# A cross-attention block on one core: two heads' scores per ScalarE instruction, some maxima on VectorE alone, fewer folded sums, and another written-out order

## The chip, the cores and the metric

The kernel runs on 1 core of a Trainium2 chip. The metric is device time in microseconds (us), the median of several executions of the whole program.

## The reference

A transformer block with cross-attention on 8 batch rows of 256 tokens, 256 keys per row, width 512, 16 heads of 32, inner width 2048, all in fp32. The mask is all ones in the inputs, but is applied.

```python
x = layer_norm(hidden, ln1_w, ln1_b)
q, k, v = x @ q_w + q_b, enc @ k_w + k_b, enc @ v_w + v_b
scores = where(mask, einsum('bhqd,bhkd->bhqk', q, k) / sqrt(32), lowest)
out = einsum('bhqk,bhkd->bhqd', softmax(scores), v) @ cproj_w + cproj_b
hidden = out + hidden
y = layer_norm(hidden, ln2_w, ln2_b)
result = hidden + gelu(y @ fc_w + fc_b) @ proj_w + proj_b
```

## The kernel before, in words

**Stages.** The eight rows are two groups `g` of four rows (1024 tokens). Each group goes through: context and input turned to feature-major layout (`c`, `x`), the projections `k`, `v`, `q`, attention in 16 units, the output projection `o`, second layer norm `y`, the first MLP product `fc`, GELU, the second MLP product `pd`. Stages of the two groups overlap.

**Products.** Every large product is done by seven products of half-size blocks (a Strassen scheme, `quad`; in the MLP, one inside the other). The products go to PSUM banks named `X`, `Y`, `W` of the quad, and other engines add them up: `L601` and `L606` copy a bank out, `L625` adds a bank to an SBUF tile. The block sums that feed them (`c0t`, `fw0i`, `z1i` and so on) are also `L625` and `L623`, on VectorE (DVE) or GpSimd (POOL). All matrix products are issued at L634; transposes by TensorE (PE) at L722, the last four at L1322.

**Attention.** A unit is one row and four heads. `scores` (its name in the program is `s` and three digits: group, four heads, row) makes 8 small matmuls, 2 chunks of 128 keys by 4 heads; a head has 32 rows, so four of them share the PE array ("row" mode). Each head's result lies in a PSUM bank of its own, two chunks of 256 columns. ScalarE (ACT) then copies the 8 pieces of 256 columns to SBUF, each with the mask as bias (`ev`, L614), into two tiles `pr` of two heads. DVE takes the maximum over the keys with a reduction that transposes 32x32 blocks (`mx`, L1033, one for each `pr`); the rest of the maximum goes over three small ACT copies (`mc`, L1039), a DVE reduction (`fold`, L1040) and a DVE transpose (`mf`, L1042), then through DRAM and back, spread over all partitions (`md`, `mm`). `less` subtracts it (POOL at L1057 in two instructions, or DVE at L1053 in one), `exp` is ACT at L1060.

Softmax sums come from a matmul with `ones`. `attend` (`av` and the digits) does it and the product with `v` in one op of small matmuls ("col" mode, four heads share the array). A unit's kind decides how: kind `z` first adds the two chunks of keys (`ss`, L625, POOL or DVE, twice 128x512) and needs 4 `ones` matmuls, kind `p` skips `ss` and needs 8. With 8 matmuls for `v` that is 12 or 16. `KINDS` gives the kind of the 16 units of each group. `inverse` and `scale` (L1083, L1085, L1086, L625) end the unit.

**Order.** Nothing is scheduled by the compiler. `PROGRAM` is a list of some 3000 words, an op each, with a letter for the engine where there is a choice (V is DVE, A is ACT, G is POOL); each engine executes its ops in that order, and waits on semaphores for what others make. `PLACES` gives the slot of SBUF or PSUM of each buffer. All DMAs are issued by SyncE (SP) in one row, loads at L588 and stores at L594.

**Start and end.** Before the first data come in, 12 small matmuls of constants (`first`, L646) are run, and 4 more (`small`) between the first transposes and the first product. At the end, the last quad's fourth product (`pd_V`) is added to an output tile on DVE (`oz`), and SP stores it (`st01`). The other rows of the second group go out in tiles `tq` of 64 KB a store (`so1`), after DVE transposes (L1349) and an addition (`out1`, L625).

**Bias.** `xb` (L1428) adds the bias of the output projection to an input tile, one instruction of 1024 columns, on POOL or DVE.

Of the kernel before, what the change touches and what calls it, by code (L numbers as in the profile page):

```python
# [127 lines left out]
rows5 c0_30:A eps_x0_1 v0_0_P2 rows4 rows6 fw0_10_0 c0t4:V v0_1_t2:V v0_0_t3:A pow_x0_1 nb_x0_1 norm_x0_11:A mk kw11
rows8 v0_1_P2 fw0_00_1 v0_0_P3 kws3:V mk~1 fw0i4_3:G fw0_10_1 cols fw0_00_0 xt0_5 v0_1_P5 fw0i4_2:V xt0_6 fw0i4_4:V
kws1:V kws2:V cols~1 k0_0_t1:A k0_1_t1:V xt0_0 k0_1_P6 v0_0_c11 xt0_7 fw0_01_0 fw0s3:V v0_1_t3:A xt0_1 fw0s1:G  # L130
fw0i5_1:G v0_1_c11 stats_x0_31 k0_0_P7 stats_x0_21 k0_1_t2:A fw0i5_2:G kw01 xt0_4 fw0_01_1 fcd0_5_False fcd0_7_False
stats_x0_00 fw0i5_3:V fw0i1_1:V fcd0_4_True fw0i7_1:G fw0i1_3:V k0_0_P6 qw00 k0_0_t2:A aggr_x0_00 fw0i7_2:V fw0i7_4:V
# [1381 lines left out]
```

## Time and profile before

| what | value |
|---|---|
| median of 3 runs (lowest to highest) | 652.07 us (650.86 to 652.34) |
| the profiled execution | 651.16 us |
| its span, first to last instruction | 649.4 us |
| PE busy | 643.4 us |
| DVE busy | 577.5 us |
| ACT busy | 346.5 us |
| POOL busy | 392.8 us |
| granted TensorE clock, mean | 1.000 |
| data moved by DMA | 144.83 MB |

Busy is the time in which an engine executes something. A matmul's end is modelled: each fp32 matmul is two instructions in the profile, and while they follow each other without a gap their modelled times overlap, so the start of one to the start of the next is the time that it takes. An idle engine costs nothing unless the last instruction waits for it. "av<-ss,ones" is an instruction that writes av and reads ss and ones; `x16` after a row is the number of instructions in it.

### The profile page before, as it was taken

To read this page: it belongs to the slowest core of one execution; us is meant where nothing else is said; L and a number is where in the kernel's file an instruction comes from. 1 tells how busy PE (TensorE), PEld (TensorE's weight loads), DVE (VectorE), ACT (ScalarE), POOL (GpSimd) and SP (SyncE) were. 2 spreads that over 40 slices of the span, in tenths; PEclk is the share of its full clock that TensorE was granted. 3 is DMA by queue.
4 is the path that set the end of the run, shared out by engine and by line. 5 is a ranking of instruction groups with operands and counts; after the bars stand their busy time and mean duration, and the time that the engine had idled before them with its cause. 6 is when DMAs were issued, how large, how long until landed. Compare 5 with 4: busy or idle time off the path is not lost.

```text
span 649.4 us, 11225 instructions
## 1 busy us (share of the span) xinstructions
PE 643.4 (99%) x3793; PEld 486.6 (75%) x3793; DVE 577.5 (89%) x985; ACT 346.5 (53%) x709; POOL 392.8 (60%) x351
## 2 busy tenths in 40 slices
PE   9999999999999999999999999999999999999997
PEld 7755464477545776787788888888888888888886
DVE  4889998999899999999999999988878777999975
ACT  2244698999999989966864746120130222523000
POOL 2643676869987997698949746325823266321244
PEclk9999999999999999999999999999999999999999
DMA  8999998668764457777877887899988989577665
GB/s 271 300 353 301 249 250 297 227 204 151 217 224 142 140 199 232 261 255 247 254 222 225 248 255 257 276 328 159 165 213 193 234 184 217 143 194 225 174 139 97
DMA packets 206713, 144.83 MB, mean 223 GB/s; under 512 B 117136, under 2 KB 167104, under 8 KB 206656
## 3 DMA queue, kind: packets, MB, share of 16 engines
q1 hardware_dynamic: 206656, 144.11, 77.9%
q8 instruction: 30, 0.49, 0.3%
q14 instruction: 27, 0.22, 0.1%
HBM read 104.10 MB, written 39.98 MB: 222 GB/s over the span
## 4 chain that ended last, share of the span: by engine, by line
PE 93%; ACT 4%; POOL 1%; DMA 1%; issue 0%; DVE 0%; ACTq 0%
PE pd_X L634 15%; PE fc_X L634 15%; PE pd_W L634 7%; PE fc_W L634 7%; PE av L634 7%; PE s L634 5%; PE q_X L634 4%; PE o_X L634 4%; PE v_X L634 4%; PE k_X L634 4%; PE fc_Y L634 4%; PE pd_Y L634 4%; PE v_W L634 2%; PE k_W L634 2%; PE o_W L634 2%; ACT pr L614 2%
## 5 line engine op out<-in xcount | busy, mean ns | idle before, releaser
L614 ACT ACTIVATE pr<-s,cols 128x256 f32<-128x256 f32 x256 | 102.9, 485 | 10.4 <-PE s L634 7.8
L1057 POOL TENSOR_TENSOR pr<-pr,mm 128x512 f32<-128x512 f32 x70 | 90.5, 1327 | 5.8 <-DMA mm<-md 5.7
L1237 ACT ACTIVATE h<-h,cols 128x256 f32<-128x256 f32 x128 | 55.2, 499 | 61.1 <-DVE h L625 45.0
L1033 DVE TRANSPOSE_TENSOR_REDUCE mx<-pr 128x32 f32<-128x1024 f32 x64 | 77.1, 1219 | 1.9 <-ACT pr L614 1.7
L1060 ACT ACTIVATE pr<-pr 128x1024 f32<-128x1024 f32 x64 | 66.5, 1061 | 11.2 <-POOL pr L1057 8.1
L625 DVE TENSOR_TENSOR h<-fc_X,h 128x512 f32<-128x512 f32 x80 | 52.5, 675 | 6.2 <-PE fc_X L634 4.9
L625 POOL TENSOR_TENSOR ss<-pr 128x512 f32<-128x512 f32 x24 | 31.5, 1322 | 14.7 <-ACT pr L1060 11.9
L625 DVE TENSOR_TENSOR h<-fc_W,h 128x512 f32<-128x512 f32 x48 | 32.0, 677 | 4.8 <-PE fc_W L634 4.1
L1053 DVE TENSOR_TENSOR pr<-pr,mm 128x1024 f32<-128x1024 f32 x29 | 35.9, 1252 | 0.0
L1039 ACT COPY mx<-mx 32x64 f32<-32x64 f32 x96 | 23.8, 249 | 14.6 <-DVE mx L1033 13.3
L623 POOL TENSOR_TENSOR z1t<-h,z1t 128x512 f32<-128x512 f32 x6 | 8.0, 1359 | 26.1 <-DMA pl<-prd 12.3
L625 POOL TENSOR_TENSOR tq<-tq,rq 128x512 f32<-128x512 f32 x8 | 10.2, 1274 | 20.7 <-DMA rq<-hd 14.4
L634 PE MATMUL pd_X<-z0i,pl 128*128 128x256 f32 x96 | 22.5, 379 | 0.0
L634 PE MATMUL fc_W<-y1i,fl 128*128 128x256 f32 x84 | 20.7, 379 | 0.0
L634 PE MATMUL pd_W<-z1i,pl 128*128 128x256 f32 x88 | 20.6, 379 | 0.0
L625 DVE TENSOR_TENSOR h<-fc_Y,h 128x512 f32<-128x512 f32 x24 | 15.9, 673 | 5.3 <-PE fc_Y L634 5.3
L634 PEld LDWEIGHTS pd_X<-z0i,pl 128*128 128x128 f32 x96 | 18.2, 190 | 2.5
L601 ACT COPY h<-fc_X 128x512 f32<-128x512 f32 x16 | 9.0, 594 | 18.5 <-PE fc_X L634 15.6
L634 PE MATMUL pd_X<-h,pl 128*128 128x256 f32 x80 | 18.9, 379 | 0.0
L811 POOL TENSOR_TENSOR rs_y<-rs_y,neg_half 128x2 f32<-128x2 f32 x8 | 10.3, 1292 | 14.2 <-DMA pl<-prd 7.7
L634 PEld LDWEIGHTS pd_W<-z1i,pl 128*128 128x128 f32 x88 | 16.7, 190 | 2.3
L625 DVE TENSOR_TENSOR po<-pd_X,po 128x256 f32<-128x256 f32 x24 | 9.9, 414 | 9.6 <-PE pd_X L634 9.5
(574 smaller groups left out, 1847.0 us busy)
## 6 DMA issues: line engine op xcount, KB each, us to landing
pl<-prd SPq DMA_DIRECT2D x65, 256.0 KB, 3.6
mm<-md SPq DMA_DIRECT2D x32, 512.0 KB, 4.2
fl<-fcd SPq DMA_DIRECT2D x40, 256.0 KB, 4.2
fw<-in_L_xattn_fc_w_dram SPq DMA_DIRECT2D x16, 256.0 KB, 3.5
hid<-in_x_dram SPq DMA_DIRECT2D x8, 512.0 KB, 6.1
pw<-in_L_xattn_proj_w_dram SPq DMA_DIRECT2D x32, 128.0 KB, 3.7
hd<-hid SPq DMA_DIRECT2D x8, 512.0 KB, 4.9
fcd<-fw0i SPq DMA_DIRECT2D x7, 512.0 KB, 6.3
```

The source lines that it names most:

```text
L601: (nc.scalar.copy if e == "ACT" else nc.vector.tensor_copy)(to(), of_())
L614: lambda e: nc.scalar.activation(to(), of_(), AF.Identity, bias=bias(), scale=1.0))
L623: nc.gpsimd.tensor_tensor(to()[:, ts(k, 512)], in0()[:, ts(k, 512)], in1()[:, ts(k, 512)], op)
L625: E[e].tensor_tensor(to(), in0(), in1(), op)
L634: nc.tensor.matmul(o(), l(), r(), start=first, stop=True, skip_group_check=True)
L811: lambda e, rs=rs: nc.gpsimd.tensor_tensor(tile_of(rs)[:, 2:4], tile_of(rs)[:, 0:2], neg_half[:, 0:2], ALU.pow), lock=True)
L1033: T.op(f"mx{u}_{h}", [("DVE", 1.126)], [(pr[h], None)], [(mx, [h])], lambda e, h=h: nc.vector.tensor_reduce(tile_of(mx)[:, 0:256].rearrang ...
L1039: lambda e, a=a: nc.scalar.copy(*(tile_of(mx)[p : p + 32, 0:256].rearrange("p (c m) -> p c m", m=8)[:, :, m : m + 2] for p, m in ((0, 2 * ...
L1053: nc.vector.tensor_tensor(p_, p_, m_[:, None, :].to_broadcast([P, 2, 512]), ALU.subtract)
L1057: E[e].tensor_tensor(p_, p_, m_, ALU.subtract)
L1060: lambda e, h=h: nc.scalar.activation(tile_of(pr[h]), tile_of(pr[h]), AF.Exp), table="exp")
L1237: lambda e, f=f, b=b, c=c: nc.scalar.activation(at(h[f][b], c), at(h[f][b], c), AF.Gelu_apprx_tanh, bias=col(c_fcb + f * 4 + c), scale=1.0 ...
```

## The change

1. PSUM is taken as four pairs of banks. A unit's scores lie in two pairs (kind `D`), and one ACT instruction takes the same chunk of both heads of a pair, 512 columns in two banks: 4 instructions (`ew`) for each unit in place of 8 (`ev`). Buffers `X`, `Y`, `W` and the like use one half of a pair, so in the lists of the changed kernel their tile has the name of the first buffer that used the pair (`ps_c0_21` where an `av` or a `k` quad is meant). `by_bank` tells the framework which instructions meet in which bank, so that the two halves of a pair do not wait for each other.
2. `MAXIMA` names 16 of the 32 units (letter v) whose maximum is finished on DVE alone: a reduction 128x32, four transposes 32x32 and a reduction 32x32, in place of 3 ACT copies, a reduction and a transpose.
3. `KINDS`: 8 units are of kind `z` in place of 16.
4. `xb` on POOL is two instructions of 512 columns; `small` writes a PSUM buffer of its own.
5. `PROGRAM` and `PLACES` are new throughout.

```diff
-SLOTS = {"Q": (45, 1024), "P": (36, 512), "H": (14, 256), "sm": (10, 32), "mx": (3, 352)}
-BANKS = ("W", "C")
+SLOTS = {"Q": (45, 1024), "P": (36, 512), "H": (14, 256), "sm": (14, 32), "mx": (3, 352)}
+BANKS = ("W", "C", "D")
...
 PROGRAM = """
-cq0_00_0 turn_c0_10_0 turn_c0_00_0 vw00 c0_10_0:A c0_00_0:V small v0_0_P1a cq0_00_1 turn_c0_00_1 c0_00_1:A cq0_01_1
+cq0_00_0 small vw00 turn_c0_10_0 c0_10_0:V turn_c0_00_0 c0_00_0:A v0_0_P1a cq0_00_1 turn_c0_10_1 turn_c0_00_1 v0_0_P1b
...
-KINDS = ("zzzzzzzzzzpppppp", "ppppppppppzzzzzz")
+KINDS = ("zppzpppzpzpppppp", "pppppppppppzpzzz")
+MAXIMA = ("vaavavvavvvvavvv", "vavvaaaavvaaaaaa")
...
+            elif b.kind == "D":
+                b.t = banks.tile([P, 1024], F32, tag=f"D{b.slot // 2}", name=b.name)
+                pairs[b.slot // 2] = None
             else:
-                b.t = banks.tile([P, 512], F32, tag=f"B{b.slot}", name=b.name)
+                s, k = divmod(b.slot, 2)
+                if pairs.get(s) is None:
+                    pairs[s] = banks.tile([P, 1024], F32, tag=f"D{s}", name=b.name)
+                b.t = pairs[s][:, ts(k, 512)]
...
-        sb = [Buf(f"s{u}_{j}", "C", 2) for j in range(4)]
+        sb = [Buf(f"s{u}_{h}", "D", 2) for h in range(2)]
...
-            for j in range(4):
-                copy(f"ev{u}_{j}{kc}", (pr[j // 2], [2 * kc + j % 2]), (sb[j], [kc]), lambda j=j, kc=kc: at(pr[j // 2], 2 * kc + j % 2),
-                     lambda j=j, kc=kc: at(sb[j], kc), 256, lambda kc=kc: col(2 * (4 * g + b) + kc))
+            for h in range(2):
+                two = lambda t: t.rearrange("p (j n) -> p j n", j=2)
+                copy(f"ew{u}_{h}{kc}", (pr[h], [2 * kc, 2 * kc + 1]), (sb[h], [kc]), lambda h=h, kc=kc, two=two: two(at(pr[h], 2 * kc, 2)),
+                     lambda h=h, kc=kc: tile_of(sb[h]).rearrange("p (j k n) -> p j k n", j=2, k=2)[:, :, kc], 512,
+                     lambda kc=kc: col(2 * (4 * g + b) + kc))
...
+        def fold(e):
+            t = tile_of(mx)
+            nc.vector.tensor_reduce(t[:, 64:96], t[:, 0:64].rearrange("p (k c) -> p c k", k=2), axis=mybir.AxisListType.X, op=ALU.max)
+            for a in range(4):
+                nc.vector.transpose(t[0:32, 96 + 32 * a : 128 + 32 * a], t[32 * a : 32 * a + 32, 64:96])
+            nc.vector.tensor_reduce(t[0:32, 320:352], t[0:32, 96:224].rearrange("p (a r) -> p r a", a=4), axis=mybir.AxisListType.X, op=ALU.max)
...
-            T.op("small", [("PE", 0.1)], [], [], lambda e: small(WARM2))
+            ps = Buf("ps_small", "C")
+            T.op("small", [("PE", 0.1)], [], [(ps, None)], lambda e: small(WARM2, tile_of(ps)))
...
+    def biased(e, h):
+        if e == "DVE":
+            v = tile_of(h).rearrange("p (i n) -> p i n", i=2)
+            nc.vector.tensor_tensor(v, v, cb.t[:, None, :].to_broadcast([P, 2, D]), ALU.add)
+            return
+        for i in range(2):
+            nc.gpsimd.tensor_tensor(at(h, i, 1, 512), at(h, i, 1, 512), cb.t, ALU.add)
```

Three places of the new order that matter below, each engine's own list.

TensorE, the product of unit 020 with `v` (op `av020`), before; the names `k1_0_Y` and the like are PSUM banks of a key projection.

```order
L634 MATMUL k1_0_Y_1043<-c1_10_967,vws2_291 128x512 x2
L634 MATMUL k1_1_X_985<-c1t2_1049,vw11_255 128x512 x2
L634 MATMUL k1_0_X_956<-c1t2_1049,vw11_255 128x512 x2
L634 MATMUL av020_1079<-ss020_1066,ones_89 32x256 x4
L634 MATMUL av020_1079<-pr020_0_794,v0_0_21_333 32x256 x2
L634 MATMUL av020_1079<-pr020_1_788,v0_0_21_333 32x256 x2
L634 MATMUL av020_1079<-pr020_0_794,v0_0_21_333 32x256 x2
L634 MATMUL av020_1079<-pr020_1_788,v0_0_21_333 32x256 x2
```

TensorE, the same op in the changed kernel; the bank has the name `ps_c0_21` of the pair's first user.

```order
L621 MATMUL ps_c0_21_270<-c1_10_850,kw01_410 128x512 x2
L621 MATMUL ps_c0_10_0_213<-c1t2_935,v0_0_21_312 128x512 x4
L621 MATMUL ps_c0_21_270<-pr020_0_751,ones_89 32x256 x2
L621 MATMUL ps_c0_21_270<-pr020_1_767,ones_89 32x256 x2
L621 MATMUL ps_c0_21_270<-pr020_0_751,ones_89 32x256 x2
L621 MATMUL ps_c0_21_270<-pr020_1_767,ones_89 32x256 x2
L621 MATMUL ps_c0_21_270<-pr020_0_751,v0_0_21_312 32x256 x2
L621 MATMUL ps_c0_21_270<-pr020_1_767,v0_0_21_312 32x256 x2
L621 MATMUL ps_c0_21_270<-pr020_0_751,v0_0_21_312 32x256 x2
L621 MATMUL ps_c0_21_270<-pr020_1_767,v0_0_21_312 32x256 x2
```

The `ones` matmuls read the scores `pr` themselves and are 8 where they were 4, and no `ss` is awaited; the op follows the same quad as before.

ScalarE, the scores of unit 020 leaving PSUM, before, up to the three small copies for its maximum.

```order
L614 ACTIVATE pr020_1_788<-s020_2_769,cols_87 128x256 x2
L614 ACTIVATE pr020_0_794<-s020_0_765,cols_87 128x256
L614 ACTIVATE pr020_1_788<-s020_3_771,cols_87 128x256 x2
L614 ACTIVATE pr020_0_794<-s020_1_767,cols_87 128x256 x2
L614 ACTIVATE pr020_0_794<-s020_0_765,cols_87 128x256
L606 ACTIVATE q0_1_21_742<-q0_1_X_650,cols_87 128x512
L606 ACTIVATE xt0_5_395<-q0_0_X_627,cols_87 128x512
L1039 COPY mx020_807<-mx020_807 32x32x2 x3
```

ScalarE, the same in the changed kernel.

```order
L601 ACTIVATE pr020_0_751<-s020_0_727,cols_87 128x512 x2
L601 ACTIVATE pr020_1_767<-s020_1_730,cols_87 128x512 x2
L593 ACTIVATE q0_1_22_770<-ps_c0_10_0_213,cols_87 128x512
L593 ACTIVATE kw01_410<-ps_c0_21_270,cols_87 128x512
L1042 COPY mx020_754<-mx020_754 32x32x2 x3
```

Eight instructions of 256 columns became four of 512, and all of one pair of heads leave before the other pair.

SyncE, the end of its list before, 64 KB stores from `tq` tiles and then the three last ones.

```order
L594 DMA out_0_dram<-tq1_1_5735 32x16x32
L594 DMA out_0_dram<-tq1_0_5633 32x16x32 x3
L594 DMA out_0_dram<-tq1_1_5735 32x16x32 x3
L594 DMA out_0_dram<-tq1_0_5633 32x16x32 x2
L594 DMA out_0_dram<-tq1_1_5735 32x16x32 x3
L594 DMA out_0_dram<-pl12_3_5631 128x2x256
L594 DMA out_0_dram<-ot0_5819 128x2x128 x2
```

SyncE, the end of its list in the changed kernel. The fifth store of the first row is the first of the half tile that `out1_10` makes, an addition that was on DVE and is on POOL now.

```order
L581 DMA out_0_dram<-tq1_1_5365 32x16x32 x5
L581 DMA out_0_dram<-tq1_0_5309 32x16x32
L581 DMA out_0_dram<-tq1_2_5299 32x16x32
L581 DMA out_0_dram<-tq1_0_5309 32x16x32
L581 DMA out_0_dram<-tq1_1_5365 32x16x32
L581 DMA out_0_dram<-tq1_0_5309 32x16x32
L581 DMA out_0_dram<-tq1_1_5365 32x16x32
L581 DMA out_0_dram<-tq1_3_5305 32x16x32
L581 DMA out_0_dram<-tq1_1_5365 32x16x32
L581 DMA out_0_dram<-tq1_0_5309 32x16x32
L581 DMA out_0_dram<-ot0_5448 128x2x128
L581 DMA out_0_dram<-tq1_0_5309 32x16x32
```

Two more rows follow, the 256 KB store from `pl14_3` and the last 128 KB store from `ot0`. Between the wait for POOL and the last store stand 12 other stores.

More of the change, by code (lines that the diff above doesn't have):

```diff
@@ L128 @@
[L128 to L132, printed above, removed]
@@ L1035, in scores @@
+            T.op(f"mx{u}_{h}", [("DVE", 1.126)], [(pr[h], None)], [(mx, [h])], lambda e, h=h, put=put: nc.vector.tensor_reduce(
+                put(),
                 tile_of(pr[h]).rearrange("p (n r) -> p n r", r=32), axis=mybir.AxisListType.X,
                 op=ALU.max, apply_transpose=True))
[L1037 to L1039 removed]
@@ L1467, in tile_xattn_block, with place, meet, by_bank @@
     proj(1, h1)
+    def place(b):
+        return {("Q", b.slot // 2, h) for h in (0, 1)} if b.kind == "Q" else {("Q", b.slot // 2, b.slot % 2)} if b.kind == "P" else {(b.kind, b.slot)}
+    def meet(o, d):
+        if d in o.deps:
+            return True
+        return any(a is not b and place(a) & place(b) for a in o.bufs for b in d.bufs
+                   if a.kind in SLOTS and b.kind in SLOTS)
+    KNOWN = mybir.DependencyInfo(mybir.DependencyClass.Sync, mybir.DependencyReason.DATA)
+    past = {}
+    def by_bank(o, made):
+        for b in {b for b, _ in o.touched if b.kind in BANKS and b.kind != "D"}:
+            tile_of(b)
+            pair, k = pairs[b.slot // 2], b.slot % 2
+            name = pair.tensor.name
+            mine = [i for i in made if any(
+                getattr(x, "bass_ap", None) is not None and x.bass_ap.tensor.name == name and x.bass_ap.offset % 1024 // 512 == k
+                for x in list(i.ins) + list(i.outs))]
+            writes = (b, True) in o.touched
+            written, read = past.setdefault((name, k), ([], []))
+            others = [(d, j) for d, j in past.get((name, 1 - k, "all"), []) if d.eng != o.eng]
+            kept = [j for d, j in others if meet(o, d)]
+            for i in mine:
+                for d, j in written + read:
+                    if d.eng != o.eng:
+                        tc.add_manual_dep(i, j.name, KNOWN, reason="same bank")
+                for d, j in others:
+                    if d in o.deps:
+                        tc.add_manual_dep(i, j.name, KNOWN, reason="operands")
+                for e in ENGINES:
+                    if e != o.eng:
+                        tc.declare_no_dep(i, group=f"{name}_{1 - k}{e}", keep=kept, reason="the pair's other bank")
+            for i in mine:
+                tc.add_to_no_dep_group(f"{name}_{k}{o.eng}", i)
+                past.setdefault((name, k, "all"), []).append((o, i))
+            last = [(o, i) for i in mine[-(4 if o.mode in ("row", "col") else 1):]]
+            if writes:
+                past[name, k] = (last, [])
+            else:
+                read.extend((o, i) for i in mine)
     order = T.run()
@@ L1471, in tile_xattn_block @@
         for o in order:
+            n = len(nc.cur_bb.bb.instructions)
             o.fn(o.eng)
+            if any(b.kind in BANKS for b in o.bufs):
+                by_bank(o, list(nc.cur_bb.bb.instructions)[n:])
 _L = "L0_xattn_"
```

684 lines of the change are left out of this document (337 added, 347 removed).

## The prediction

> **What bounds the kernel now.** I read the page's busy times first, then PE's time by stages, then PE's waits: an engine that is busy all through leaves little to an edit that does not change its own work. From the page (busy us, share of the span, instructions):
>
> ```profile
> PE 643.4 (99%) x3793; PEld 486.6 (75%) x3793; DVE 577.5 (89%) x985; ACT 346.5 (53%) x709; POOL 392.8 (60%) x351
> ```
>
> From the view by stages (stretch, its length, busy time of PE, weight loads, DVE, ACT, POOL, then clock, DMA share, GB/s):
>
> ```profile
> 60.00:110.00 50.00, 49.30 (x264) 25.32 (x263) 47.02 (x82) 37.98 (x88) 30.71 (x29) 1.00 0.95 268
> 110.00:165.00 55.00, 54.71 (x412) 35.80 (x410) 51.52 (x93) 53.12 (x112) 44.89 (x37) 1.00 0.76 195
> 165.00:215.00 50.00, 49.76 (x417) 25.57 (x410) 46.91 (x81) 48.88 (x104) 43.77 (x30) 1.00 0.55 179
> 275.00:320.00 45.00, 44.78 (x342) 33.91 (x335) 43.77 (x77) 32.07 (x68) 40.34 (x42) 1.00 0.81 261
> 400.00:500.00 100.00, 100.00 (x465) 87.79 (x464) 85.87 (x144) 17.97 (x31) 43.73 (x40) 1.00 0.91 234
> ```
>
> PE is idle for 649.4 - 643.4 = 6.0 us. The four attention stages hold 0.70 + 0.29 + 0.24 + 0.22 = 1.45 of it, the start 0.98 and the time after PE's last instruction 3.58 (both by rows below). ACT, nearly full from 110 to 215 us, still lets PE run. So this is a PE-bound kernel, and the question is what the change does to PE's list.
>
> A short wait does not show as idle, since the modelled end of the matmul before covers it; it shows as a start that comes late. Rows of the timeline (start, us, instruction, count):
>
> ```profile
> 105.28 3.70 PE L634 MATMUL k_X<-c1t,kws 128*128 128x512 f32 x8
> 109.68 1.96 PE L634 MATMUL k_W<-c1t,xt 128*128 128x512 f32 x4 [0.70 <-DVE mx L1042]
> ...
> 209.39 3.62 PE L634 MATMUL o_X<-q,att 128*128 128x256 f32 x16
> 213.15 1.67 PE L634 MATMUL s<-v,k 32*128 32x256 f32 x16
> 214.75 1.99 PE L634 MATMUL o_X<-ows,a0t 128*128 128x256 f32 x8
> 216.68 1.15 PE L634 MATMUL s<-vws,k 32*128 32x256 f32 x16
> 217.75 1.99 PE L634 MATMUL o_X<-ows,a0t 128*128 128x256 f32 x8
> ...
> 307.90 1.03 PE L634 MATMUL fc_X<-y0t,xn_x 128*128 128x256 f32 x4
> 309.15 0.64 PE L634 MATMUL av<-ss,ones 128*32 128x256 f32 x8 [0.22 <-ACT pr L614]
> ...
> 314.35 1.03 PE L634 MATMUL fc_X<-y0i,vw 128*128 128x256 f32 x4
> 315.21 1.03 PE L634 MATMUL fc_X<-y0i,q 128*128 128x256 f32 x4
> 316.17 0.64 PE L634 MATMUL av<-ss,ones 128*32 128x256 f32 x8
> ```
>
> Undisturbed, an instruction of 256 columns takes 100 us / 465 = 0.215 us (the stage from 400 to 500), and an `s` op 217.75 - 216.68 = 1.07 us. The `s` op at 213.15 takes 1.60. I laid all 504 matrix operations between the first transpose at 3.74 us and the last end at 645.82 end to end, each with the median start-to-start time of its kind and neighbours: 636.3 of 642.1 us (an estimate from the timeline). About 5.7 us are lost to waits then, some 0.8 of them in the first 12 us.
>
> **The change part by part.**
>
> *Unit kinds.* A product of kind z alone between full-size products, and one of kind p:
>
> ```profile
> 338.95 0.64 PE L634 MATMUL av<-ss,ones 128*32 128x256 f32 x8
> 339.41 1.05 PE L634 MATMUL av<-pr,qws 128*32 128x256 f32 x16
> 340.39 1.13 PE L634 MATMUL fc_X<-y,fl 128*128 128x256 f32 x4
> 341.36 1.03 PE L634 MATMUL fc_W<-y0i,fl 128*128 128x256 f32 x4
> ...
> 172.85 1.07 PE L634 MATMUL av<-pr,ones 128*32 128x256 f32 x16
> 173.74 1.05 PE L634 MATMUL av<-pr,vws 128*32 128x256 f32 x16
> 174.72 1.98 PE L634 MATMUL q_X<-x1t,qws 128*128 128x512 f32 x4
> ```
>
> z takes 340.39 - 338.95 = 1.44 us, p takes 174.72 - 172.85 = 1.87. The change turns 8 of 16 z units into p: 8 x 0.43 = +3.44 us, all of it on PE, which has no idle time to take it. What it saves (16 additions `ss`) is on POOL and DVE.
>
> *Switches of mode.* A small op between full ones costs its neighbours something: 316.17 - 315.21 = 0.96 where 315.21 - 314.35 = 0.86, so 0.10 going in, and 341.36 - 340.39 = 0.97, 0.11 for the first product after it. In the lists, runs of `s` and `av` between full products number 34 before and 33 now, and two `av` or `s` side by side are 31 pairs in place of 30, which saves about 0.14 of drain. -0.2 - 0.14 = -0.35 us. [...]
>
> *Scores in pairs, maxima on DVE.* ACT and DVE, from the groups and the timeline:
>
> ```profile
> L614 ACT ACTIVATE pr<-s,cols 128x256 f32<-128x256 f32 x256 | 102.9, 485 | 10.4 <-PE s L634 7.8 <-issue 1.2 <-ACT xn_y L822 0.6
> L1039 ACT COPY mx<-mx 32x64 f32<-32x64 f32 x96 | 23.8, 249 | 14.6 <-DVE mx L1033 13.3
> L1040 DVE TENSOR_REDUCE mx<-mx 32x32 f32<-32x256 f32 x32 | 12.5, 390 | 3.3 <-ACT mx L1039 3.1
> L1042 DVE STREAM_TRANSPOSE mx<-mx 32x32 f32<-32x32 f32 x32 | 5.8, 184 | 0.2
> L614 ACT ACTIVATE att<-att,cols 128x512 f32<-128x512 f32 x16 | 11.3, 718 | 1.0 <-DVE att L625 0.9
> ...
> 186.66 3.03 ACT L614 ACTIVATE pr<-s,cols 128x256 f32<-128x256 f32 x8
> ```
>
> Eight evacuations take 3.03 us in a row. Four of 512 columns take at most 4 x 0.72 = 2.9 and, overlapped as the eight are (485 ns each, but 3.03 for eight, so 0.11 less apiece), 4 x 0.61 = 2.4. No row shows one instruction over two banks; between 2.3 and 3.0 I take 2.4, nearest to the row of the same form. It saves ACT some 0.6 us a unit, and 3 x 0.25 in each of 16 units, all off PE's path. DVE pays for the latter with 3 transposes and a reduction more, 3 x 0.18 + 0.39 = 0.9 us in 16 units, of which the `ss` and `less` ops that left DVE (6 and 7 in the list) give back most. What reaches PE is the wait for it. The waits above whose releaser is a score copy or a maximum: 109.68 - 105.28 - 8 x 0.43 = 0.96, at 209.39 3.76 - 16 x 0.215 - 0.10 = 0.22, at 213.15 1.60 - 1.07 = 0.53, at 307.90 1.25 - 0.96 = 0.29. Together 2.0 us.
>
> *The new order.* It moves every engine's list, so these waits would fall elsewhere anyway. Slack that an earlier copy leaves can be spent by putting the product earlier. I take -1.4, two thirds of the 2.0, for all waits, with ends of -4.9 (nothing lost after the start: 5.7 - 0.8) and +3 (half as much again as now).
>
> *Start.* All 32 small matmul instructions come before the first transposes now.
>
> ```profile
> 0.98 2.82 PE L646 MATMUL first<-warm 128*64 128x64 f32 x24 [0.98 <-DVE warm L641]
> 3.74 1.10 PE L722 MATMUL ps_c<-ident,cq 128*128 128x128 f32 x4
> 4.77 0.68 PE L646 MATMUL first<-warm 128*64 128x64 f32 x8
> 5.38 1.13 PE L634 MATMUL v_X<-vw,c 128*128 128x256 f32 x4
> ```
>
> The 8 cost 5.38 - 4.77 = 0.61 us; now the transposes wait for them and the copies after the transposes are exposed, up to 0.6 late, of which a wait for loads before 12 us takes back half: +0.3, between 0 and 0.7.
>
> *End.* The last store waits for `oz`, and SP issues in order.
>
> ```profile
> 638.37 2.75 POOL L623 TENSOR_TENSOR z1i<-z1t,z1i 128x512 f32<-128x512 f32 x2 [1.31 <-PE pd_W L634]
> 638.78 4.14 SPq L594 DMA_DIRECT2D out_dram<-tq  x8
> 644.86 0.39 SPq L594 DMA_DIRECT2D out_dram<-pl  x1
> ...
> 643.87 1.95 PE L634 MATMUL pd_V<-pl,z1i 128*128 128x128 f32 x16
> 645.86 0.42 DVE L625 TENSOR_TENSOR ot<-pd_V,ot 128x256 f32<-128x256 f32 x1 [0.70 <-PE pd_V L634]
> ```
>
> Before, SP was idle from 642.9 to 644.86. Now 12 stores stand between POOL's `out1_10` and the last one: at 4.14 / 8 = 0.52 that is 6.2 us. POOL does `z1i4_4` (the 2.75 us above) after it and before the last product, which starts 1.95 us before PE's end, so `out1_10` is done at the latest 4.7 us before that end. The last store would then go out 1.5 us after the end, where `oz` allows 0.46: 1.0 late. I take 0.0, the case in which POOL is ahead by that much, with an upper end of +1.0.
>
> *Nothing.* `xb` in two instructions on POOL and the new slots: off PE's path, POOL being 60% busy; if that cover is gone, the layer norm `y` waits, and it is in the +3.
>
> Sum: 3.44 - 0.35 - 1.4 + 0.3 + 0.0 = +2.0 us. On the profiled execution of 651.16 us (span 649.4 and 1.8 around it) that is 653.2. The median of the runs is 652.07, 0.9 above, so I forecast 654.1.
>
> **The rivals.**
>
> *Same time.* The new order loses 2.1 to 4.7 us less to waits than the old. For it: the waits listed above have one cause each, and the change shortens just these two chains. Against it: 3.4 us more work on a full engine must be found in 5.7 us of loss, 0.8 of which is the start. Time: 3.1 - 2.5 + 0.3 = +0.9, or 653.0, within 1.3 us of now.
>
> *Faster.* From 60 to 320 us PE never waits: the copies and the maxima come so early that every `s` finds its banks free and every `av` its scores. That is 4.9 us back: 3.1 - 4.9 + 0.3 = -1.5, or 650.6. It decides from a rest of losses under 1.5 us. Against it: DVE is 94% busy from 60 to 165 us and hands PE something in every stage.
>
> *The pair is held.* One instruction reads two banks, so neither comes free before both heads' two chunks are out (2 x 0.61 = 1.2 us), where a bank came free after its own two copies (0.76); the next quad that wants a half waits 0.45 longer. It matters only where PE is that close, as in the four places above: 4 x 0.45 = 1.8 in place of the 1.4 gained: 3.1 + 1.8 + 0.3 = +5.2, or 657.3. Against it: the last bank is free earlier (2.4 for 3.0). [...] This trace has no pair and cannot show the price.
>
> **How the numbers follow.** A measurement of this kernel tells about 0.2% from no change, 1.3 us. Forecast (+1.3 to +4): 0.47. Pair held, or the end late and the new order no better (+4 to +7): 0.16. Same: 0.28. Faster: 0.09. So slower 0.63, same 0.28, faster 0.09. The range leaves out 0.1 at each side: from -0.7 (651.4), inside the case of the same time, to +5.3 (657.4), the pair held.
>
> **What would show it.** In the changed profile 24 `av` ops of 1.87 and 8 of 1.44 us, so PE busy 3 us more, near 646.5; 128 score copies of 0.6 to 0.72 us; ACT busy 30 us less; idle time of PE between 60 and 320 us near 0.7. If the copies take over 0.9 us, the pair is dear. If PE's first product starts by 5.4 us, the start term is wrong; if SP's last store is issued over 0.6 us after PE's end, the end term is. A time under 651.4 means that PE's losses were more than I could lay out end to end, or that PE's work is less than its list.

## The result and the profile after

| | before | changed |
|---|---|---|
| time, median of four runs (us) | 652.21 (650.86 to 652.35) | 667.76 (665.05 to 670.19) |
| ratio, 95% interval | | 1.0231 (1.0204 to 1.0258): slower |
| profiled execution: time, span (us) | 651.16, 649.4 | 669.1, 667.3 |

The forecast was 654.1 and the range ended at 657.4. Here and below, medians are over all executions, while ratios leave out an execution more than 1.5% above the fastest of its kernel. First the page of the changed kernel, busy times:

```profile
PE 650.2 (97%) x3857; PEld 490.1 (73%) x3857; DVE 575.9 (86%) x1003; ACT 322.5 (48%) x547; POOL 453.8 (68%) x394
```

and the stage that lost most (stretch, length, busy time of PE, weight loads, DVE, ACT, POOL, then clock, DMA share, GB/s):

```profile
165.00:215.00 50.00, 42.85 (x336) 20.87 (x332) 46.47 (x77) 33.31 (x49) 38.98 (x31) 0.90 0.41 134
```

PE was idle for 0.24 us between 165 and 215 us and is now idle for 7.15, at a lower clock. The view of PE's waits (us in total, times, longest) names one event:

```profile
PE ps_c L621 <- ACT qws L593: 7.1, 1, 7.1
```

The timeline around it, one engine after the other (PE, ACT, DVE, POOL):

```profile
184.49 1.88 PE L621 MATMUL ps_c<-x1t,v 128*128 128x512 f32 x4
193.47 3.78 PE L621 MATMUL ps_c<-x,k 128*128 128x512 f32 x4 [7.11 <-ACT qws L593]
197.19 2.09 PE L621 MATMUL s<-vw,k 32*128 32x256 f32 x16
...
187.48 1.06 ACT L1063 ACTIVATE pr<-pr 128x1024 f32<-128x1024 f32 x1 [6.68 <-DVE pr L1056]
191.79 1.06 ACT L1063 ACTIVATE pr<-pr 128x1024 f32<-128x1024 f32 x1 [3.25 <-DVE pr L1056]
192.75 0.67 ACT L593 ACTIVATE qws<-ps_c,cols 128x512 f32<-128x512 f32 x1
...
177.77 9.68 DVE L1056 TENSOR_TENSOR pr<-pr,mm 128x1024 f32<-128x1024 f32 x1
...
159.21 4.98 POOL L1060 TENSOR_TENSOR pr<-pr,mm 128x512 f32<-128x512 f32 x4 [1.87 <-DMA mm<-md]
...
176.49 2.54 POOL L1060 TENSOR_TENSOR pr<-pr,mm 128x512 f32<-128x512 f32 x2
178.95 2.53 POOL L610 TENSOR_TENSOR x1t<-x,x1t 128x512 f32<-128x512 f32 x2
181.40 2.53 POOL L1060 TENSOR_TENSOR pr<-pr,mm 128x512 f32<-128x512 f32 x2
183.84 2.53 POOL L1420 TENSOR_TENSOR hid<-hid,cb 128x512 f32<-128x512 f32 x2
188.19 2.48 POOL L1060 TENSOR_TENSOR pr<-pr,mm 128x512 f32<-128x512 f32 x2 [1.82 <-DMA mm<-md]
```

Read it from below. POOL adds and subtracts without a gap until 186.37 (183.84 + 2.53); its row began at 159.21 and has 22 instructions, of which DVE meets the 16th. DVE's subtraction of the maxima, `less023_0`, comes up at 177.77, takes 9.68 us where 1.2 is usual, and ends 1.08 us after POOL's row has ended. ACT's exponential waits for it; the copy `q1_0_t3` (`qws<-ps_c`) stands behind two exponentials in ACT's list; PE's next product of the query projection, `q1_0_P3`, waits for that copy. After the wait four matmuls take 3.78 us instead of 1.88 and the scores 2.09 instead of 1.15: from 192 to 198 us the clock was granted at 0.50.

Laid end to end with the same durations as in the prediction, PE's list is 639.4 us now (636.3 before: +3.1), and what it loses to waits is 20.7 (5.5 before: +15.2); these sums are estimates from the timelines. The one event holds 10.2 of these: 7.3 at `q1_0_P3`, 2.9 in the slow products behind it. Many small waits hold the other 5.0.

In the kernel before, DVE and POOL met at the same place like this (timeline, DVE, then POOL; then two of the groups):

```profile
179.51 2.34 DVE L1053 TENSOR_TENSOR pr<-pr,mm 128x1024 f32<-128x1024 f32 x2
...
180.89 3.35 POOL L623 TENSOR_TENSOR x1t<-x,x1t 128x512 f32<-128x512 f32 x2 [2.00 <-DVE pr L1053]
```

```profile
L1057 POOL TENSOR_TENSOR pr<-pr,mm 128x512 f32<-128x512 f32 x70 | 90.5, 1327 | 5.8 <-DMA mm<-md 5.7
L1053 DVE TENSOR_TENSOR pr<-pr,mm 128x1024 f32<-128x1024 f32 x29 | 35.9, 1252 | 0.0
```

POOL had run out of work at 178.89 and waited for DVE, so DVE's two subtractions met no row and took 1.2 us each. The new order gives POOL seven subtractions more (14 instructions), and DVE seven fewer. The groups of the changed kernel:

```profile
L601 ACT ACTIVATE pr<-s,cols 128x512 f32<-128x512 f32 x128 | 80.5, 687 | 35.0 <-PE s L621 31.3 <-PE o_W L621 2.3 <-PE q_X L621 0.6
L1060 POOL TENSOR_TENSOR pr<-pr,mm 128x512 f32<-128x512 f32 x84 | 109.3, 1332 | 17.2 <-DMA mm<-md 13.4 <-PE q_X L621 2.0 <-issue 1.2
L1056 DVE TENSOR_TENSOR pr<-pr,mm 128x1024 f32<-128x1024 f32 x22 | 39.1, 1777 | 3.9 <-DMA mm<-md 3.9
```

The mean of DVE's subtraction went from 1252 to 1777 ns: nothing about the instruction changed, and 8.5 of the 11.6 us that the 22 lost are the one at 177.77.

### The profile page after: what moved, and what is told of

Same layout as the page of the kernel before. It is cut to its first block, busy times and chain, and to the rows that moved or that the text cites. A ratio compares the mean times of both kernels' runs of the same rounds, so it can differ in the third digit from the quotient of the medians.

```text
span 667.3 us, 11275 instructions
## 1 busy us (share of the span) xinstructions
PE 650.2 (97%) x3857; PEld 490.1 (73%) x3857; DVE 575.9 (86%) x1003; ACT 322.5 (48%) x547; POOL 453.8 (68%) x394
## 4 chain that ended last, share of the span: by engine, by line
PE 76%; DVE 12%; DMA 5%; POOL 3%; issue 2%; SPq 1%; ACT 1%; DVEq 0%; ACTq 0%; POOLq 0%
PE fc_Y L621 26%; PE fc_X L621 12%; PE fc_W L621 12%; PE ps_c L621 9%; PE s L621 3%; PE av L621 3%; DVE pr L1056 3%; DMA mm<-md 3%; DVE mx L1026 2%; PE k_W L621 2%; PE o_W L621 2%; PE q_X L621 2%; PE v_X L621 2%; PE ps_small L621 2%; POOL pr L1060 1%
## 5 line engine op out<-in xcount | busy, mean ns | idle before, releaser
L1060 POOL TENSOR_TENSOR pr<-pr,mm 128x512 f32<-128x512 f32 x84 | 109.3, 1332 | 17.2 <-DMA mm<-md 13.4
L601 ACT ACTIVATE pr<-s,cols 128x512 f32<-128x512 f32 x128 | 80.5, 687 | 35.0 <-PE s L621 31.3
L612 DVE TENSOR_TENSOR h<-fc_Y,h 128x512 f32<-128x512 f32 x75 | 49.8, 678 | 5.7 <-PE fc_Y L621 5.5
L1056 DVE TENSOR_TENSOR pr<-pr,mm 128x1024 f32<-128x1024 f32 x22 | 39.1, 1777 | 3.9 <-DMA mm<-md 3.9
L1420 POOL TENSOR_TENSOR hid<-hid,cb 128x512 f32<-128x512 f32 x14 | 22.7, 1648 | 6.3 <-DMA hid<-in_x_dram 6.3
L612 POOL TENSOR_TENSOR ss<-pr 128x512 f32<-128x512 f32 x14 | 18.1, 1311 | 6.6 <-ACT pr L1063 6.6
L621 PE MATMUL fc_Y<-z0i,pl 128*128 128x256 f32 x88 | 20.5, 379 | 0.0
L612 DVE TENSOR_TENSOR h<-fc_X,h 128x512 f32<-128x512 f32 x25 | 16.9, 680 | 2.8 <-PE fc_X L621 2.6
L610 POOL TENSOR_TENSOR z0t<-h,h 128x512 f32<-128x512 f32 x10 | 15.5, 1569 | 4.8 <-ACT xn_y L809 4.8
L621 PEld LDWEIGHTS fc_Y<-z0i,pl 128*128 128x128 f32 x88 | 16.7, 190 | 2.3
L621 PE MATMUL fc_Y<-y1i,fl 128*128 128x256 f32 x72 | 18.0, 379 | 0.0
L612 POOL TENSOR_TENSOR tq<-tq,rq 128x512 f32<-128x512 f32 x8 | 11.6, 1455 | 7.4 <-DVE tq L1352 5.0
L798 POOL TENSOR_TENSOR rs_y<-rs_y,neg_half 128x2 f32<-128x2 f32 x8 | 8.4, 1052 | 11.9 <-DVE rs_y L795 6.3
```

The source lines that it names most:

```text
L601: lambda e: nc.scalar.activation(to(), of_(), AF.Identity, bias=bias(), scale=1.0))
L610: nc.gpsimd.tensor_tensor(to()[:, ts(k, 512)], in0()[:, ts(k, 512)], in1()[:, ts(k, 512)], op)
L612: E[e].tensor_tensor(to(), in0(), in1(), op)
L621: nc.tensor.matmul(o(), l(), r(), start=first, stop=True, skip_group_check=True)
L798: lambda e, rs=rs: nc.gpsimd.tensor_tensor(tile_of(rs)[:, 2:4], tile_of(rs)[:, 0:2], neg_half[:, 0:2], ALU.pow), lock=True)
L1056: nc.vector.tensor_tensor(p_, p_, m_[:, None, :].to_broadcast([P, 2, 512]), ALU.subtract)
```

## The experiments

The theory after the trace: DVE's additions of two SBUF operands and POOL's share something, and DVE is not served while POOL's row goes on. The texts on record call that something the port; the runs show who waits for whom and how long, not what it is. The rivals: the data were late; ACT's order; or many small waits. Ratios are to the kernel before on the same chip.

**Four edits of one word or two** (a word is an operation's name; V is DVE, G POOL, A ACT).

*both_on_pool*

```diff
-less023_0:V ... less011_1:V
+less023_0:G ... less011_1:G
```

> The changed kernel with two subtractions of attention moved from DVE to POOL (less023_0 and less011_1): in its trace DVE's less023_0 takes 9.68 us instead of 1.2, from 177.77 until POOL's unbroken row of eight additions and subtractions ends at 186.37, and less011_1 takes 2.18. Theory (DVE is starved by POOL's row, and the one wait of PE that this makes, 7.1 us, with the TensorE clock that is low after it, 2.9 us by the start-to-start times, is most of the loss): the subtraction costs 2.5 us on POOL, the copy q1_0_t3 follows the product before it at once, PE's wait there falls from 7.1 to about 0.8 and no product after it is slow: 9 to 10 us less than the changed kernel, 658 to 659. Rival (the data were late, not the port): POOL now waits in DVE's place, and the wait of PE and the time stay, 666 to 668. Rival (many small waits: PE is caught by the next late step at once): less than 4 us are gained, 664 or more.

Measured: 671.01 us, ratio 1.0267 (1.0226 to 1.0308): no gain. The subtraction no longer waits, the next two-operand sum of DVE does (timeline of DVE, then PE's waits):

```profile
184.27 15.12 DVE L612 TENSOR_TENSOR vws<-q,v 128x512 f32<-128x512 f32 x1
```

```profile
PE s L621 <- DVE qws L612: 9.0, 1, 9.0
```

POOL's row, longer by the two subtractions and without the pause that stood at 186, ended at 198.84, and DVE was held until then. The forecast of the time failed, since I moved work to the engine whose row does the holding. The cause it tested stands: these operands were not late and had no maxima to wait for.

*one_on_pool*

```diff
-less023_0:V
+less023_0:G
```

> The changed kernel with less023_0 alone moved from DVE to POOL. Theory (any DVE subtraction that meets POOL's unbroken row is held to its end): POOL's row grows by 2.5 us and ends near 188.8; less011_1, which DVE now reaches near 180, takes 9 us in place of 2.2 and ends near 190; the copy q1_0_t3 stands behind its exponential and runs at about 191 in place of 192.75: PE still waits 5 to 6 us there, and the time is 665 to 667. Rival (only this one subtraction was hit, by chance or by late data): the wait is gone, 658 to 659.

Measured: 674.42 us (664.65 to 675.86), ratio 1.0261 (1.0178 to 1.0343); the time is above the 665 to 667 expected, and the rival's 658 to 659 is out. As the theory said, `less011_1` is held now, and longer than I reckoned, as POOL found no pause at 186 this time:

```profile
181.41 16.02 DVE L1056 TENSOR_TENSOR pr<-pr,mm 128x1024 f32<-128x1024 f32 x1
```

*xb_later*

```diff
-xb0_3:G ... less013_1:G
+less013_1:G xb0_3:G
```

> The changed kernel with POOL's bias addition xb0_3 (two instructions, 2.5 us) put behind the subtraction less013_1, so that POOL's row ends 2.5 us earlier and nothing else moves. Theory (the starved subtraction ends when the row ends): less023_0 ends 2.5 us earlier, near 185.0, PE's wait falls from 7.1 to about 4.6 us, the time by 2 to 3 us to about 665. Rival (the subtraction waited for its data): its end does not move, and neither does the time, 667 to 668.

Measured: 662.78 us, ratio 1.0134 (1.0099 to 1.0168). Two instructions less in the row, and the hold is shorter by 9.68 - 7.69 = 2.0 us, PE's wait by 3.5:

```profile
179.09 7.69 DVE L1056 TENSOR_TENSOR pr<-pr,mm 128x1024 f32<-128x1024 f32 x1
```

The hold ends with the row, as the theory says; late data are out. PE's wait fell by more than the hold, as `less011_1`, 2.18 us long in the changed kernel, met no row here and took 1.18; the time, 5.0 us lower, fell by more than this explains.

*t3_before_exp*

```diff
-exp023_0 exp011_1 x1t4:G q1_0_t3:A
+q1_0_t3:A exp023_0 exp011_1 x1t4:G
```

> The changed kernel with the copy q1_0_t3 put ahead of the two exponentials exp023_0 and exp011_1 in ACT's list; DVE's and POOL's lists stay. Theory (the starved subtraction reaches PE only through ACT's order): less023_0 still takes 9 to 10 us, the copy runs at about 186.3, PE's wait of 7.1 us falls to about 0.8 and the low clock after it is gone, but the product av011 then waits for the late exponentials, some 2 to 3 us: 6 to 8 us less, 660 to 662. Rival (the late exponentials are what counts, whatever the order): av023 and av011 take over the whole wait, and the time stays within 2 us, 666 to 668.

Measured: 666.54 us, ratio 1.0184 (1.0148 to 1.0220): not the 660 to 662 of the theory, and at the rival's edge. PE's products ran on, and PE then waited for something I had not listed, DVE's sum `vw` behind the held subtraction:

```profile
194.43 1.86 PE L621 MATMUL s<-vw,k 32*128 32x256 f32 x16 [4.33 <-DVE vw L612]
```

So ACT's order only chose which result PE missed first. Everything queued behind the held instruction on DVE was late.

**Which rows hold.** In the six traces so far I took every DVE instruction that ran over 0.15 us past its kind's usual time while POOL's row went on after the current instruction. I counted POOL's instructions up to the one that DVE met, from the row's last gap or from the last one that DVE itself had delayed (counted from gaps alone, two rows of eighteen let DVE in). With ten or fewer, some 160 cases, DVE got in at the first boundary, but for two that came free 0.06 us ahead of one and got in at the next. With twelve it got in in two of three cases; with fifteen or more it lost in all ten. The expectations below start the count later and say nine and fourteen. So the length of the row should decide. Three tests of it:

*row_cut*: one wait more, POOL's sum `x1t2` for DVE's maximum `mx013_1`, no work moved.

```diff
+CUTS = [("x1t2", "mx013_1")]
+            for a, b in CUTS:
+                if a == o.name:
+                    tc.add_manual_dep(made[a][0], made[b][-1].name, KNOWN, reason="cut")
```

> The changed kernel with one wait more: POOL's sum x1t2 waits for DVE's maximum mx013_1, which ends near 174.7 us, so that POOL's row has one gap of some 0.7 us about three instructions before DVE's subtraction less023_0 comes free at 177.8. No work moves. Theory (in the six traces so far DVE took the port at the first boundary between two POOL instructions whenever POOL's unbroken row was at most 9 long, and lost every boundary up to the row's end from 14 on): after the gap the row is short, less023_0 takes at most 2.5 us, less011_1 too, PE's wait of 7.1 us before q1_0_P3 falls under 1.5 us and no low clock follows: 9 us less, 657 to 660. Rival (POOL's queue as such holds the port, whatever the length of its row): less023_0 still takes 8 to 10 us, time 667 to 669. Rival (another late step takes the place): 664 or more.

Measured: 661.29 us (658.37 to 670.02), ratio 1.0105 (1.0069 to 1.0141). The gap of 0.84 us in POOL's row is there and DVE is served in time (POOL, then DVE):

```profile
175.90 2.52 POOL L612 TENSOR_TENSOR x1t<-x,x1t 128x512 f32<-128x512 f32 x2 [0.84 <-DVE mx L1028]
...
178.78 1.94 DVE L1058 TENSOR_TENSOR pr<-pr,mm 128x1024 f32<-128x1024 f32 x1
```

A wait of POOL, added, makes the kernel 6 to 8 us faster (by the medians and by the ratios). Four of six runs were at 658.4 to 661.4, two at 668.7 and 670.0.

*port_rows* and *port_rows2* measure the hold by itself: rows of POOL additions, and one DVE instruction that comes free at the end of the row's k-th.

```diff
+g = made(lambda: nc.gpsimd.tensor_tensor(many[:, to : to + w], ga[:, :w], gb[:, :w], ALU.add))
+v = made(lambda: nc.vector.tensor_tensor(vo[:, :512], va[:, :512], vb[:, :512], ALU.add))
+tc.add_manual_dep(v, row[k - 1].name, KNOWN, reason="place in the row")
```

> The disputed cost by itself: nothing of the block is computed, the output is filled with zeros, and POOL runs rows of k + 8 additions of two SBUF operands (128x512, then 128x256) while one DVE instruction comes free at the end of POOL's k-th; k goes from 2 to 24. Theory (the length of POOL's unbroken row decides): DVE's addition of two SBUF operands waits at most one POOL instruction, 1.3 us, up to k = 9, and to the row's end, 9 to 10 us, from k = 14; with a gap cut three instructions before, at k = 16, it waits at most one. DVE's instructions with one SBUF operand or one in PSUM wait for nothing. With 128x256, where a POOL instruction takes 0.7 us, the same count decides if it is the queue, about k = 20 if it is the time of some 14 us. Rival (first come, first served at each boundary): never more than one POOL instruction at any k. Rival (POOL always wins while its queue holds anything): to the row's end at every k.

> The disputed cost by itself, second part (nothing of the block is computed; the output is zeros). Theory (from a row of about fifteen on, POOL's next instruction always comes before DVE's, until the row ends): the switch from at most 1.3 us to the row's end lies at one k between 14 and 16 and repeats; with 24 instructions behind it DVE waits some 30 us, with one behind it 2.5; a single link, one POOL instruction that waits for the one before it, three places ahead gives DVE the port at the first boundary. DVE's transposes, reductions and copies with one SBUF operand, if they need the shared port, wait 10 us as the sum with a constant did (10.0), or nothing (the STREAM_TRANSPOSE and TRANSPOSE_TENSOR_REDUCE rows of the kernel keep their times beside POOL, so these should not wait). Rival (a fixed waiting time after which DVE is served): 10 us with 24 behind it, too.

The first, timeline of DVE: k = 9, 14 and 16 with 128x512; k = 12 and 16 with 128x256 on POOL; then at k = 16 a sum with a constant, an operand in PSUM, the cut row, and a row in which each instruction waits for the one before:

```profile
82.49 1.73 DVE L63 TENSOR_TENSOR vo<-va,vb 128x512 f32<-128x512 f32 x1 [11.13 <-POOL many L46]
...
210.61 1.73 DVE L63 TENSOR_TENSOR vo<-va,vb 128x512 f32<-128x512 f32 x1 [17.23 <-POOL many L46]
...
241.11 10.27 DVE L63 TENSOR_TENSOR vo<-va,vb 128x512 f32<-128x512 f32 x1 [19.67 <-POOL many L46]
...
347.96 1.20 DVE L63 TENSOR_TENSOR vo<-va,vb 128x512 f32<-128x512 f32 x1 [8.32 <-POOL many L46]
...
365.51 5.96 DVE L63 TENSOR_TENSOR vo<-va,vb 128x512 f32<-128x512 f32 x1 [11.04 <-POOL many L46]
...
434.91 10.01 DVE L57 TENSOR_SCALAR vo<-va 128x512 f32<-128x512 f32 x1 [19.67 <-POOL many L46]
...
465.13 0.69 DVE L59 TENSOR_TENSOR vo<-acc,vb 128x512 f32<-128x512 f32 x1 [19.67 <-POOL many L46]
...
526.19 1.73 DVE L63 TENSOR_TENSOR vo<-va,vb 128x512 f32<-128x512 f32 x1 [3.81 <-POOL many L46]
...
558.49 0.69 DVE L63 TENSOR_TENSOR vo<-va,vb 128x512 f32<-128x512 f32 x1 [21.47 <-POOL many L46]
```

The second: k = 14; k = 20 with 24 more behind it; with one link three places ahead; and at k = 20 a transpose, a copy and a copy into PSUM:

```profile
20.25 10.28 DVE L57 TENSOR_TENSOR vo<-va,vb 128x512 f32<-128x512 f32 x1 [12.36 <-POOL many L49]
...
144.64 29.79 DVE L57 TENSOR_TENSOR vo<-va,vb 128x512 f32<-128x512 f32 x1 [24.55 <-POOL many L49]
...
243.29 1.73 DVE L57 TENSOR_TENSOR vo<-va,vb 128x512 f32<-128x512 f32 x1 [24.68 <-POOL many L49]
...
315.68 0.71 DVE L58 STREAM_TRANSPOSE vo<-va 128x512 f32<-128x512 f32 x1 [24.55 <-POOL many L49]
...
420.49 10.01 DVE L61 COPY vo<-va 128x512 f32<-128x512 f32 x1 [24.55 <-POOL many L49]
...
525.47 0.69 DVE L64 COPY acc<-va 128x512 f32<-128x512 f32 x1 [24.55 <-POOL many L49]
```

What each DVE row shows beyond its own 0.69 us is the wait: about one POOL instruction (1.0) or all that is left of the row (9.6; with 24 behind, 29.1). The rivals fall: neither first come, first served, nor POOL ahead at every k, nor a fixed waiting time. With half the size the switch comes between 12 and 16 too, at about half the elapsed time (8.3 to 11.0 us of idle DVE before it, against 17.2 to 19.7), so in these rows the count decides and not the time. It is not sharp: k = 14 was served in one kernel and held in the other. One more expectation failed: the sum with a constant, which has one operand in SBUF, was to wait for nothing and was held like the others. Why a long row keeps DVE out is not shown.

**The other terms.**

*row_cut_ew_split*

```diff
+            for j in range(2):
+                nc.scalar.activation(to()[:, j], of_()[:, j], AF.Identity, bias=bias(), scale=1.0)
```

> The kernel row_cut with each of the 128 score copies over two banks (0.69 us) split into two copies of 256 columns, one bank each, so that ACT has some 20 to 25 us more to do and a quad's last score comes out 0.4 to 0.6 us later, as in the kernel before. Theory of the prediction (the paired copies shorten waits of PE by a part of 1.4 us): 0.5 to 1.5 us more than row_cut. Rival (the pair is held, which cost PE): up to 2 us less than row_cut. Rival (the copies are off PE's path by now): within 0.5 us of row_cut.

Measured: 661.55 us against row_cut's 661.29; ratios 1.0120 (1.0091 to 1.0149) and 1.0105. ACT was busy 18 us more and the time did not move beyond the noise: the ratios differ by 0.15%, with an uncertainty of 0.46% (3 us). All three expectations lie within that, so what the paired copies are worth to PE stays open.

*kinds_alone*

```diff
-KINDS = ("zzzzzzzzzzpppppp", "ppppppppppzzzzzz")
+KINDS = ("zppzpppzpzpppppp", "pppppppppppzpzzz")
-ss020_0 ss020_1 ... ss111_1
```

> The kernel before with the changed kernel's table of unit kinds alone: 8 of its 16 units z become p, their 16 additions ss fall away, every other word keeps its place. Term of the prediction: 8 x 0.43 = 3.4 us more work of PE, none of it hidden; waits after it move by less than 1 us: 3 to 4 us more than before, PE busy near 647. Rival (the products wait anyway, so that longer ones cost nothing): 0 to 1 us more. Rival (POOL and DVE relieved of 16 additions give PE shorter waits): 1 to 2.5 us more.

Measured: 658.89 us against 653.3, ratio 1.0080 (1.0055 to 1.0104): 3.6 to 6.8 us, around 5.2, above the 3 to 4 expected. Laid end to end, PE's list is some 3.7 us longer (an estimate from the two timelines), near the forecast's 3.4; the rest is waits, in an order that was written for the shorter products. The longest, in PE's waits, was 0.7 before:

```profile
PE k_W L633 <- DVE mx L1041: 1.8, 1, 1.8
```

*row_cut_z*

```diff
-KINDS = ("zppzpppzpzpppppp", "pppppppppppzpzzz")
+KINDS = ("zzzzzzzzpzpppppp", "ppppppppppzzzzzz")
+ss020_0 ss020_1 ... ss111_1
```

> The kernel row_cut with the table of unit kinds undone as far as free slots allow: 7 of the 8 units go back from p to z, and 14 additions ss stand again between their exponentials and their products (on POOL or DVE as in the kernel before). By the work alone, 7 x 0.43 = 3.0 us less of PE than row_cut. Theory (longer products cost their work and, as kinds_alone showed with 5.6 against 3.4, something in waits): 3 to 5 us less than row_cut, about 657. Rival (the additions that come back fill POOL and DVE again and cost what the products save): within 1 us of row_cut. Rival (POOL's rows grow and a DVE instruction is held again): as slow as row_cut or slower, with a DVE instruction of over 5 us in the trace.

Measured: 694.62 us, ratio 1.0607 (1.0557 to 1.0656), on the side of the third expectation and far beyond it. PE waits 17.9 us for additions `ss` that stand in full lists, and one subtraction of DVE is held again, by another of POOL's rows:

```profile
240.21 12.81 DVE L1060 TENSOR_TENSOR pr<-pr,mm 128x1024 f32<-128x1024 f32 x1
```

It says nothing of the price of a kind, only that the new order has no room for these additions.

*links* and *links_before*: every operation on POOL waits for the POOL instruction before it, so that no row is long.

```diff
+            if o.eng == "POOL":
+                if behind is not None:
+                    tc.add_manual_dep(new[0], behind.name, KNOWN, reason="link")
+                behind = new[-1]
```

> The changed kernel with its lists as they are, and one wait more for every operation on POOL: its first instruction waits for the last of the operation before it on POOL, which costs about 0.12 us of POOL's time each (the gap of 78 ns in the row of POOL instructions that wait for one another, and the overlap of 42 ns that is lost), some 25 us of POOL in all, and leaves no unbroken row of more than a few instructions. Theory (the row's length decides, and that alone made the large wait): no DVE instruction takes over 2.6 us where 1.2 is usual; PE's wait of 7.1 us and the low clock go, in every execution, so that no run is above 663: 656 to 660. Rival (the large wait has another cause, which row_cut met by chance): a run in three is at 667 to 671, as with row_cut. Rival (slower POOL now hands PE its data late): 661 to 666 in all runs.

> The same links put into the kernel before. Theory: its trace has no DVE instruction that meets a row of POOL of more than four, so nothing is to be gained there; POOL, 60% busy, has room for 25 us more: the same time as before within 1 us. Rival (rows matter in executions that no profile shows): 1 us or more faster, with less spread. Rival (POOL's data become late): 1 to 3 us slower.

Measured: links 663.47 us (659.44 to 666.18), ratio 1.0128 (1.0085 to 1.0171); links_before 664.21, ratio 1.0146 (1.0109 to 1.0183). No DVE instruction lost more than 1.1 us to POOL in either trace, but the times are on the side of the rivals, in the second run far beyond it. My price for a link was wrong by what follows from it: in the kernel before, where there was nothing to gain, the links cost 9.5 us. PE's waits of links_before:

```profile
PE k_W L634 <- DVE mx L1042: 2.5, 1, 2.5
...
PE av L634 <- POOL pr L1057: 1.0, 1, 1.0
```

POOL was 60% busy, and still 15 us more of it reached PE.

*few_links*: 13 links, one where a row would pass eight instructions.

```diff
+LINKS = ("c1t3", "less021_0", "less023_1", "x1t4", "less122_1", "a0t4", "less130_1",
+         "y0i2_2", "y0t4", "fc007_21", "fc007_22", "y1t1", "z1t4_3")
-                if behind is not None:
+                if o.name in LINKS:
```

> The changed kernel with 13 links in place of 288: the first instruction of 13 operations on POOL waits for the POOL instruction before it (about 0.12 us each, 1.6 us in all), each where a row of the changed kernel's trace would pass eight instructions. Theory (a row that is cut in time gives DVE the port, and the cost of links was POOL's lateness, 25 us of it): no DVE instruction is held over 2.6 us, the wait of 7.1 us and the low clock are gone without the one-sided cost of 288 links: 657 to 660, a little under row_cut, and no run at 667 to 671, where two of six of row_cut's were. Rival (those two runs had another cause): one or two of six runs at 667 or more again. Rival (a link delays what PE waits for, however few there are): 661 to 664 as with all links.

Measured: 660.23 us (658.50 to 662.48), ratio 1.0113 (1.0079 to 1.0146). All six runs lie together, at the upper edge of the theory's 657 to 660; why two of row_cut's were late is not shown. The longest hold is smaller but not under the 2.6 us expected: one subtraction took 3.00 us. PE's wait of 7.1 us is gone. Against the changed kernel's 1.0231 the held instruction is worth 0.0118 (about 7.7 us, give or take 2.8). The longest of PE's waits:

```profile
PE o_W L624 <- DMA kws<-in_L_xattn_fc_w_dram: 2.4, 1, 2.4
```

No version here beats the kernel before.

## Why the prediction was wrong, step by step

- *Nothing.* This step failed. It put `xb` "and the new slots: off PE's path, POOL being 60% busy", and gave the lost cover a place in the +3. The 60% is a mean over the span: in the changed kernel POOL's row from 159 to 186 us has no gap, and such a row holds DVE, through which it reached PE: 10.2 of the 17.9 us between the two profiled executions, or about 7.7 by the times of few_links. I asked of POOL's new instructions whether POOL had time, not whether DVE could run beside them. `xb` is only the end of that row (two instructions; moving them took 2.0 us off the hold). Ten of the 22 are subtractions, and the seven that went from DVE to POOL stood in the prediction as relief for DVE, with no price on POOL. The before trace had the sign of it, DVE rows lengthened beside POOL, but none by over 1.1 us, and no row that went on past DVE there had more than five instructions by then. None of my rivals had this mechanism. PE's busy time, 650.2 where I said 646.5, is in part stretched by the low clock: it is 647.2 in row_cut, where the clock stayed at 1.00.
- *The waits, -1.4 between -4.9 and +3.* The sign was wrong too. Beside the held instruction the trace has 5.0 us more of small waits. The two kinds of wait that I named did not shrink: as idle time of PE they were 0.70 for a maximum and 0.22 for a score copy, and are 0.4 and 1.4 now. In few_links neither is among PE's waits, and others are in their place, the longest 2.4 for a DMA.

```profile
PE fc_W L621 <- ACT pr L601: 1.4, 1, 1.4
...
PE av L621 <- DVE mx L1032: 0.4, 1, 0.4
```

  PE's idle time between 60 and 320 us, for which I gave near 0.7, is 11.9. few_links leaves 1.13% (7.4 us) over the kernel before; kinds_alone explains 0.80% (5.2), and the rest, 0.33% with an uncertainty of 0.42%, is not told from nothing. What share of the small waits each rearranged piece causes was not separated.
- *Unit kinds, +3.44.* The work was right. A p unit in the changed trace takes 312.34 - 310.47 = 1.87, as forecast:

```profile
310.47 1.07 PE L621 MATMUL av<-pr,ones 128*32 128x256 f32 x16
311.36 1.05 PE L621 MATMUL av<-pr,xt 128*32 128x256 f32 x16
312.34 1.13 PE L621 MATMUL fc_W<-y0i,xt 128*128 128x256 f32 x4
```

  The whole list grew by 3.1, the sum of this step and the switches (-0.35). The 0.14 among these agrees with the timeline of the kernel before, where a p unit between two others takes 202.94 - 201.21 = 1.73 us against 1.87 alone; that a drain is the cause is not shown. Alone in the old order they cost 5.2, the rest as waits.
- *Scores in pairs.* The size was right: 0.687 us a copy, inside 0.6 to 0.72. ACT fell by 24 us where I said 30. The worth to PE, hoped for in the waits, is not measurable (row_cut_ew_split), and neither is the loss of 1.8 us that the rival of the held pair gave. The wait of 1.4 us for a paired copy is the one place where the pair may have cost PE something; with the copies split there are still 1.1 us of it, in two waits, so the pairing is not shown to be its cause.
- *Start, +0.3.* PE's first product starts at 5.82 us where it started at 5.38: 0.44. *End, 0.0.* The last store goes out at 664.53, 0.49 after PE's last matmul at 664.04, so POOL's `out1_10`, done at 655.51, was early enough.

```profile
5.82 1.13 PE L621 MATMUL v_X<-vw,c 128*128 128x256 f32 x4 [0.46 <-ACT c L588]
...
664.53 0.39 SPq L581 DMA_DIRECT2D out_dram<-ot  x1
```

## What to carry to other kernels

A mean busy share says nothing of an engine's longest unbroken row, and in these runs that row of POOL is what DVE met: POOL was 68% busy in the changed kernel, with a row of 27.2 us without a gap, and one subtraction of DVE took 9.68 us where 1.2 is usual. Look for DVE instructions that outlast their kind, and try one wait that cuts the row where POOL may wait (row_cut: 1.94 us). In an order fitted to its durations, a change of length can cost waits on top of its own size (here 5.2 us for 3.4 of work), and work taken off one engine's list is not free on the other (both_on_pool: PE's longest wait 9.0 us, 7.1 in the changed kernel).

## What the runs showed of the hardware

- Who was held beside a long row of POOL's additions (port_rows at k = 16, port_rows2 at k = 20): DVE's additions of two SBUF operands (10.27 us), sums with a constant and copies from SBUF to SBUF (10.01); not its transposes (0.71), its reductions (0.69 and 0.71), its fills (0.48), nor an addition with one operand in PSUM or a copy into PSUM (0.69).
- How long: an addition of 0.69 us that came free early in the row took 1.73 (k = 9), 1.0 more, where a POOL instruction takes 1.2. Late in the row it took 10.27 with eight instructions behind it (k = 16) and 29.79 with 24 (k = 20): 9.6 and 29.1 more, the whole rest of the row.
- A POOL row in which each instruction waits for the one before (25.89 us for 19, 1.36 each; without these waits 27.33 for 22, 1.24 each) cost DVE nothing: 0.69 us at k = 16. With a single such wait, three places ahead, DVE got in after one POOL instruction (1.73 at k = 20).
- PE's granted clock in the changed kernel was 0.65 from 188 to 192 us, inside the wait of 7.11 us, 0.50 from 192 to 198 and 1.00 again from 200 on. In few_links, after a wait of 2.38 us that ended at 260.70, it was 0.95 from 260 to 262, 0.50 from 262 to 264 and 0.70 from 264 to 266, and the second and third product took 1.75 and 1.91 us instead of 1.03. links_before, whose longest wait was 2.5 us, has a mean clock of 0.997; row_cut, links and kinds_alone, whose longest were 1.3, 1.7 and 1.8, have 1.000.

```profile
260.70 1.10 PE L624 MATMUL o_W<-y,kws 128*128 128x256 f32 x4 [2.38 <-DMA kws<-in_L_xattn_fc_w_dram]
261.64 1.75 PE L624 MATMUL o_W<-y,fl 128*128 128x256 f32 x4
263.18 1.91 PE L624 MATMUL av<-y,fl 128*128 128x256 f32 x4
```
